# One list of lags, ranks by stage behind the first phase, and three small networks moved behind the last expert block

## The chip, the cores and the metric

The kernel runs on one core of one Trainium2 chip. The metric is the device time of one execution in microseconds, the median of several runs. The core's engines are PE (TensorE: matrix products and transpositions, with PEld for the loading of weights), DVE (VectorE), ACT (ScalarE), POOL (GpSimd) and SP, which here only issues DMAs. Each engine carries out its instructions strictly in the order in which they are written; an instruction that waits holds up everything behind it on its engine.

## The reference, cut to what matters

Two layers of a network over x of 32 sequences with 256 tokens of width 256 (8192 tokens), all in float32, 16 heads of 16. What the change touches begins in the last part of the first layer.

```python
# layer 0: modulated linear attention, gated cosine attention, adapter, attention block (the first phase), then
h = layer_norm(x); x = x + moe(h)          # 8 experts of width 1024, two choices a token, 2048 slots an expert, ReLU
# layer 1, "second linear" and the kernel attention
y = clip(((x * styles) @ weight.T) * dcoefs + bias, -256, 256)       # styles, dcoefs: one vector a sequence
q, k, v = y @ Wq.T + bq, y @ Wk.T + bk, y @ Wv.T + bv
q = q / norm(q); k = k / norm(k)           # norms over the whole tensor, all sequences together
s = sum(phi(q) * phi(k))                   # phi: exp of a small product, one s for each token and head
x = x + s * v / s
# layer 1, conditioning
h = ln(ln(x, pw[pathway]), cp[compartment]); t = ln(x, tm[time]); s = ln(x, ms[scale])   # gains, offsets gathered by token
m, n, r = (x + mlp_ln(state) for state in (memory, noise, resource))                     # one vector a sequence
w = softmax(aw)
c = ln(silu(concat(w0*h, w1*t, w2*m, w3*n, w4*r, w5*s) @ W1 + b1) @ W2 + b2)
# layer 1, feed-forward: 256 to 1024 to 256, both weights passed through ten butterfly stages
x = x + butterfly(gelu(butterfly(c @ W_exp + b_exp) + up_bias)) @ W_con + b_con + down_bias
```

## The kernel before, in words

**The planner.** The program is not written in the order in which it is executed. Each piece of work is a `Part`, a generator that yields an engine and a cost in microseconds ahead of the instructions it then writes (`yield PE, 1.75`). It can also yield a pause (`None, 2.0`), a join with another Part, a turn of a ring of buffers or of a set of lanes, a Part to be started beside it, and a change of rank. `side_by_side(parts, lags)` (L98) simulates the engines with these costs: of all steps that are due it takes the one with the earliest start, and among equal starts the one with the lowest rank; where a Part passes from one engine to another, a lag is added by the engine that it comes from. A step with two choices (`(ACT, 0.7), (DVE, 0.75)`) goes to the engine where it ends first. The order so found is the order of the instructions on each engine. It is fixed before anything runs, so a cost or a lag that is not that of the chip changes only the order. `DVE2` is a DVE operation that also takes the "port" which POOL operations take, so that the planner lays neither beside the other.

A Part's rank begins as its place in the list of Parts. `yield "stage", name` sets it to that place plus `STAGES[name]`; in the kernel before only the first phase does this. `yield "rank", B` puts the feed-forward of a sequence behind all earlier steps of others.

The first phase is planned by `side_by_side(..., LAGS_A)`, with a lag of 0.08 us, or 0.3 behind PE. All that follows is planned in a single call with `LAGS_D`, 0.2 us behind every engine:

```python
[routed, weights_part, *loads[:2], matrices, *blocks, *loads[2:], table_part, *first_parts, square_part, norm_part]
+ [Part(answer_out(b, first_parts[-3] if b < 2 else norm_part, [norm_part])) for b in range(B)]
```

**What follows the first phase**, in order of time:

- `expert_block` (32 blocks, 4 for each expert, 512 slots each; 4 lanes). POOL gathers the tokens (xg, L1600), PE transposes them (L1610), then 8 groups of bh (L1644) with a ReLU on ACT or DVE (L1633), then by (L1659), the sum ysb on DVE (L1665), the gate of the slot, and `add_to_tokens`: a POOL issue for each 128 slots that adds rows to `rrows` in DRAM (L1567), one at a time by `scatter_turn`.
- `matrices`, the butterflies: the 20 stages on w_eff and w_con, six DVE2 operations each (L1701 to L1707), which lie beside the expert blocks; at its end PE transposes w_con in four groups (L1761) and DVE copies them.
- `small_tables` joins `matrices` first. It loads rows, multiplies the phi weights (L1930, L1940), scales the conditioning weights iw1 on ACT and adds parts of them to wcat on POOL, and then carries out the three small networks for memory, noise and resource one after another, each with its loads, PE (L2008, L2017, L2034), ACT, DVE and POOL steps. A last group on PE (L2050) makes bvec of them.
- `answer(b)` (32 sequences, 6 lanes), the second linear: it waits for all blocks and scatters, loads x back, transposes it (xmT), multiplies by cw, clips to yT and stores that; 28 sequences add to a gram matrix, 4 make their squares directly.
- `squares` and `norms`: the norms of q and k over everything (L2069 to L2099). qs, a product with ones, rstd on POOL, scaled phi weights (wa_aq, ab_aq), aphr and phs. Every sequence's phi product waits for them. `norms` joins all `answer`s, `squares`, `small_tables` and `matrices`.
- `answer_out(b)` (4 lanes), the last stretch, one chain for each sequence:
  - dyT and x are loaded, and POOL gathers six rows of gains and offsets (`tables`, ga and gc, L2106);
  - v by wav on PE and DVE (L2152); the phi product on PE (L312) and ph on DVE (L2164), exp on ACT (L2167), sums on DVE (L2171 to L2181), x + v on POOL (L2183);
  - statistics (L361, L362) on DVE, rstd on POOL (L256, L262) and the norm on DVE (L284): xh; then t and s by two POOL operations each (L2118, L2120), and beside them hh by two on DVE, the second norm, h by two on DVE, its transposition on PE (L292) and its copy cT_h on DVE (L2205);
  - the wcat product on PE (L2218) over x, t, s and h; Silu on ACT (L2227), iw2 on PE (L312), u on DVE (L2235), its norm un, transposition and zT on DVE (L2246);
  - the feed-forward: four groups of dh (L2269) with Gelu on ACT (L2259), do (L2283), the sum xo on DVE (L2289) and the store.

Names such as `mm`, `sh` and `big` are rings of buffers, `mm` those in PSUM.

Of the kernel before, what the change touches and what calls it, by code (L numbers as in the profile page):

```python
# [93 lines left out]
LAGS_A = defaultdict(lambda: 0.08, {PE: 0.3})  # L94
LAGS_D = defaultdict(lambda: 0.2)


def side_by_side(parts, lags):  # L98
# [112 lines left out]
    "residual out": 0.0,  # L211
}
# [3 lines left out]
def network(ctx: ExitStack, tc: tile.TileContext, a: dict, out: bass.AP):  # L216
# [1140 lines left out]
    with tc.manual_schedule():  # L1357
        side_by_side(
            [tables[False, "k"], *first_sequences, Part(moderate()), Part(routed_early(first_sequences))]
            + [tables[False, "o"], constants_part, tables[True, "k"], tables[True, "o"], adapter_part, tables[False, "c"]]  # L1360
            + [Part(numbers())],
            LAGS_A,
        )
    with tc.If(nc.values_load(again[0:1, 0:1]) > 0):
        sequences = [Part(sequence(b, True)) for b in range(B)]
        side_by_side([*sequences, Part(routed_early(sequences))], LAGS_A)
# [184 lines left out]
    def slot_gates(j0):  # L1551
        for p in rest:
            yield "join", p
        yield None, 2.0
        yield POOL, 1.1 * QT_
        for j in range(j0, j0 + QT_):
            nc.gpsimd.indirect_dma_start(
                gslot[:, j : j + 1], None, gbuf[:, :], bass.IndirectOffsetOnAxis(ap=grow[:, j : j + 1], axis=0)
            )
        yield None, 2.0  # L1560

    def add_to_tokens(y, j0, n):

        for t in range(n):
            yield scatter_turn
            yield POOL, 1.6
            nc.gpsimd.indirect_dma_start(  # L1567
                rrows[:, :], bass.IndirectOffsetOnAxis(ap=row[:, j0 + t : j0 + t + 1], axis=0), y[:, t, :], None,
                compute_op=ALU.add,
            )  # L1570
            yield None, 3.0
            yield "back", scatter_turn
        yield back("sh")
# [15 lines left out]
    def expert_block(e, blk, w, loaded, routed):  # L1589
        yield lanes_b  # L1590
# [13 lines left out]
        yield None, 2.0  # L1604
        hT = []
# [17 lines left out]
        yield hid_turn  # L1623
        hid = []

        def relu(f, ps):
            bcol = cols[:, C_B1 + 8 * e + f : C_B1 + 8 * e + f + 1]
            o = hid[f // 4][:, f % 4, :]
            engine = yield (ACT, 0.7), (DVE, 0.75)
            if engine == DVE:  # L1630
                nc.vector.tensor_scalar(o, ps, bcol, 0.0, ALU.add, ALU.max)
            else:
                nc.scalar.activation(o, ps, AF.Relu, bias=bcol)  # L1633
            yield back("mm")
# [16 lines left out]
        for p in rs:  # L1651
            yield "join", p
        for t0 in range(0, QT_, 2):
# [57 lines left out]
    def butterflies(after):  # L1711
# [33 lines left out]
        for st in reversed(range(NST)):  # L1745
# [9 lines left out]
            yield back("big")  # L1755
        for f in range(0, 8, 2):
# [7 lines left out]
            yield DVE, 0.7  # L1764
            nc.vector.tensor_copy(w_con[:, f : f + 2, :], ps)
# [21 lines left out]
    def answer(b):  # L1787
# [3 lines left out]
        for p in scatters:  # L1791
            yield "join", p
        yield lanes_c
# [24 lines left out]
        if b < NG:  # L1818

# [80 lines left out]
    def small_tables():  # L1900

        yield "join", weights_part
        yield "join", matrices
        yield SP, 0.1
        nc.sync.dma_start(rowsD, a["rows_d"][:, :N_ROWS_D].to_broadcast([P, N_ROWS_D]))
        bb = yield from get("sh", "bb")
        yield SP, 0.1
        nc.sync.dma_start(
            bb.rearrange("p t d -> p (t d)"), a["rows_d"][:, N_ROWS_D : N_ROWS_D + 2 * D].to_broadcast([P, 2 * D])
        )  # L1910
        yield None, 2.5
        yield DVE2, 0.5
        nc.vector.tensor_add(bcon, bb[:, 0, :], bb[:, 1, :])
        yield back("sh")
        yield POOL, 0.1
        nc.gpsimd.memset(qacc, 0.0)
# [3 lines left out]
        nc.sync.dma_start(blk, a["ablk"].rearrange("(k p) m -> p k m", p=P))  # L1920
        for n in ("aq", "ak"):
            nat = yield from get("sh", "nat")
            yield SP, 0.1
            nc.sync.dma_start(nat, a[n].rearrange("(k p) i -> p k i", p=P))
            yield None, 2.5
# [20 lines left out]


# [7 lines left out]
        condin = {}  # L1955
        for n, src, k in (("mem", "condT", P), ("noi", "noiT", 64), ("res", "resT", 32)):
            if n == "mem":
                condin[n] = condT
            else:
                condin[n] = wD.tile([k, B], F, name="ci_" + n)  # L1960
                yield SP, 0.1
                nc.sync.dma_start(condin[n], a[src])
# [27 lines left out]
        vT = {}  # L1990
        for n in ("mem", "noi", "res"):
            ci = condin[n]
            k = ci.shape[0]
            m1 = yield from get("sh", "m1", [k, D])
            m2 = yield from get("sh", "m2")
            rb = yield from get("sh", "rb", [B, D])
            yield SP, 0.1
            nc.sync.dma_start(m1, a[n + "W1"])
            yield SP, 0.1
            nc.sync.dma_start(m2, a[n + "W2"].rearrange("(k p) n -> p k n", p=P))  # L2000
            o, w_ = ROWS_S[n + "b2"]
            yield SP, 0.1
            nc.sync.dma_start(rb, a["rows_s"][:, o : o + w_].to_broadcast([B, w_]))
            yield None, 2.5
            ps = yield from get("mm", "mm", TS)
            yield PE, 0.4
            for m in range(2):
                nc.tensor.matmul(ps[:, m, :B], m1[:, m * P : (m + 1) * P], ci, start=True, stop=True)  # L2008
            hT = yield from get("sh", "mhT", [P, 2, B])
            yield ACT, 1.8  # L2010
            for m in range(2):
                nc.scalar.activation(hT[:, m, :], ps[:, m, :B], AF.Silu, bias=col(n + "b1", m))
            yield back("mm")
            ps = yield from get("mm", "mm", TS)
            yield PE, 0.9
            for c in range(2):
                nc.tensor.matmul(ps[:B, 0, :], hT[:, c, :], m2[:, c, :], start=(c == 0), stop=(c == 1))  # L2017
            u = yield from get("sh", "mu", [B, D])
            st = sm.tile([B, 6], F, name="mst")
            mv = sm.tile([B, 2], F, name="mmv")  # L2020
            rstd = sm.tile([B, 1], F, name="mrs")
            yield DVE, 1.1
            nc.vector.tensor_add(u, ps[:B, 0, :], rb)
            nc.vector.bn_stats(st, u)
            nc.vector.bn_aggr(mv, st)
            yield back("mm")
            yield POOL, 0.8
            rsqrt(rstd, mv[:, 1:2], 1, LN_EPS)
            yield DVE, 0.4
            nc.vector.tensor_scalar(u, u, mv[:, 0:1], rstd, ALU.subtract, ALU.mult)  # L2030
            ps = yield from get("mm", "mm", TS)
            yield PE, 0.3
            for c in range(2):
                nc.tensor.transpose(ps[:, c, :B], u[:, c * P : (c + 1) * P], ident[:B, :B])  # L2034
            vT[n] = wD.tile([P, 2, B], F, name="vT_" + n)
            yield DVE, 0.3
            for c in range(2):
                nc.vector.tensor_scalar(
                    vT[n][:, c, :], ps[:, c, :B], col(n + "g", c), col(n + "be", c), ALU.mult, ALU.add
                )  # L2040
            yield back("mm")
            for _ in range(5):
                yield back("sh")
# [57 lines left out]
    def tables(b, gt):  # L2101
        for n, q in (("pw", 0), ("ct", 1), ("ms", 2)):
# [20 lines left out]
    def side_part(xh, gt, n, i, name, into):  # L2123
        x = yield from modulated(POOL, name, xh, gt, n, i, 1.3)
# [3 lines left out]
    def whole(x2, into):  # L2128
        into["x"] = yield from transposed(x2, "cT_x")

    def answer_out(b, begin, before):

        yield "join", begin
        yield lanes_d
# [21 lines left out]


# [9 lines left out]
        nc.scalar.activation(ph, ph, AF.Exp)  # L2167
        s_ = sm.tile([P, 2, H], F, name="s_")
# [17 lines left out]

        cT = {}
# [8 lines left out]
        hh = yield from modulated(DVE, "hh", xh, gt, "pw", 0, 0.7)  # L2196
        h2 = yield from layer_norm(sm, hh, "h2")
# [6 lines left out]
        yield DVE, 0.7  # L2204
        nc.vector.tensor_copy(cT["h"], ps)  # L2205
        yield back("mm")
        yield back("sh")
        for p in (px, pt, ps_):
# [35 lines left out]
        yield DVE, 0.9  # L2244
        for c in range(2):
            nc.vector.tensor_scalar(  # L2246
                zT[:, c, :], ps[:, c, :], col("intg", c), col("intbe", c), ALU.mult, ALU.add
            )
# [3 lines left out]
        yield "rank", B  # L2252
        gT = yield from get("big", "gT", [P, 8, S])

        def gelu(ps, f0):
            yield ACT, 1.0 if f0 else 2.2
# [20 lines left out]
        for p in gs:  # L2277
            yield "join", p
        ps = yield from get("mm", "do", [P, 2, D])
# [30 lines left out]
    norm_part = Part(norms([*first_parts, square_part, table_part, matrices]))  # L2310
    with tc.manual_schedule():
# [3 lines left out]
            LAGS_D,  # L2315
# [124 lines left out]
```

## Time and profile before

| what | value |
|---|---|
| median of 3 runs | 3712.47 us (3708.94 to 3715.06) |
| profiled execution, its own time | 3708.21 us |
| its span in the profile | 3706.5 us |
| mean granted TensorE clock | 0.978 |
| PE busy | 3488.0 us, 94% of the span |
| PEld busy | 2564.0 us, 69% |
| DVE busy | 2467.3 us, 67% |
| ACT busy | 1805.9 us, 49% |
| POOL busy | 1887.7 us, 51% |
| DMA | 241.44 MB, mean 65 GB/s |

The times of single instructions come from one profiled execution. A line of the timeline reads: start, duration, engine, source line, operation, output<-inputs, shapes, and in brackets the idle time of the engine before the instruction and what ended it. A line of the list of waits reads: instruction that waited <- instruction that released it: total us, how often, largest.

### The profile page before, as it was taken

The numbers are of one execution on the slowest core, as the hardware profiler recorded it, in microseconds if no ns is written. First come the engines' busy times: TensorE is split into PE (matmuls) and PEld (weight loads), VectorE is DVE, ScalarE is ACT, GpSimd is POOL, SyncE is SP. The second block draws the span as 40 slices with busy tenths as digits, with TensorE's granted clock in tenths as the row PEclk, the third lists the DMA queues.
The fourth block names the chain that finished last, engine by engine and source line by source line (L and its number), as shares of the span: only waits on it lengthen the run. The fifth ranks groups of instructions, "written<-read, shape, count | busy, mean of one in ns | idle before, by whom it ended". The sixth has DMA issues, their size and how long they took to land. (4 is left out here: it accounts for less than half of the span.)

```text
span 3706.5 us, 55576 instructions
## 1 busy us (share of the span) xinstructions
PE 3488.0 (94%) x22001; PEld 2564.0 (69%) x22001; DVE 2467.3 (67%) x4039; ACT 1805.9 (49%) x2790; POOL 1887.7 (51%) x1515
## 2 busy tenths in 40 slices
PE   3899999999999999969999999999998999999999
PEld 2566666666666666646666666666787888888888
DVE  7999999999999999747654540011346656565554
ACT  2677777777777777732222222222333333333333
POOL 4546555555555554426546665553024656565553
PEclk7999999999999999979999999999999999999999
DMA  1011010100100111032334334222341323233321
GB/s 64 16 34 33 31 31 31 31 31 27 29 25 28 31 31 37 25 123 69 101 83 106 97 76 91 44 37 40 131 168 43 105 93 116 94 97 97 120 94 43
DMA packets 136495, 241.44 MB, mean 65 GB/s; under 512 B 19265, under 2 KB 80897, under 8 KB 133666
## 3 DMA queue, kind: packets, MB, share of 16 engines
q0 software_dynamic: 48128, 100.77, 11.2%
q1 hardware_dynamic: 87954, 136.51, 11.1%
q8 instruction: 176, 2.88, 0.3%
q14 instruction: 93, 0.76, 0.1%
q10 hardware_dynamic: 144, 0.52, 0.0%
HBM read 187.25 MB, written 50.48 MB: 64 GB/s over the span
## 5 line engine op out<-in xcount | busy, mean ns | idle before, releaser
L1028 ACT ACTIVATE pt<-sc 128x2048 f32<-128x2048 f32 x256 | 481.5, 1881 | 108.6 <-PE sc L1019 105.7
L1633 ACT ACTIVATE hid<-bh,cols 128x512 f32<-128x512 f32 x256 | 175.3, 688 | 600.5 <-PE bh L1644 600.5
L1659 PE MATMUL by<-w,hid 128*128 128x256 f32 x2048 | 454.5, 380 | 3.2 <-DVE ysb L1665 3.2
L1644 PE MATMUL bh<-ehT,w 128*128 128x512 f32 x1024 | 451.5, 594 | 0.8 <-DVE ysb L1665 0.8
L1659 PEld LDWEIGHTS by<-w,hid 128*128 128x128 f32 x2048 | 387.7, 191 | 67.8 <-issue 14.3
L262 POOL TENSOR_TENSOR n<-n,negh 128x32 f32<-128x32 f32 x64 | 364.8, 5700 | 5.3
L1567 POOL DMA_INDIRECT rrows<-ysb,row x128 | 220.3, 1721 | 259.7 <-DMA rrows<-ysb,row 146.2
L1665 DVE TENSOR_TENSOR ysb<-by,b 128x512 f32<-128x512 f32 x64 | 44.0, 688 | 456.9 <-PE by L1659 382.7
L1644 PEld LDWEIGHTS bh<-ehT,w 128*128 128x128 f32 x1024 | 194.8, 191 | 220.8 <-issue 214.7
L256 POOL TENSOR_SCALAR rstd<-mv 128x2 f32<-128x2 f32 x160 | 62.7, 392 | 506.9 <-DVE mv L362 500.5
L835 DVE TENSOR_TENSOR hprod<-hprod 128x1024 f32<-128x1024 f32 (+2 forms) x384 | 313.3, 816 | 7.1
L1019 PE MATMUL sc<-qT,kT 32*128 32x256 f32 x4096 | 294.2, 401 | 19.4 <-ACT pt L1028 17.8
L827 DVE TENSOR_TENSOR hprod<-hex,kk 128x2048 f32<-128x2048 f32 x128 | 292.2, 2283 | 0.0
L1001 PE MATMUL av<-pt,vaug 128*32 128x256 f32 x4096 | 271.8, 385 | 5.6 <-ACT pt L1028 5.6
L1019 PEld LDWEIGHTS sc<-qT,kT 32*128 32x128 f32 x4096 | 185.4, 184 | 93.7 <-ACT pt L1028 42.7
L2269 PE MATMUL dh<-zT,w_eff 128*128 128x256 f32 x1024 | 235.9, 379 | 0.5 <-DVE zT L2246 0.5
L2283 PE MATMUL do<-w_con,gT 128*128 128x256 f32 x1024 | 230.9, 379 | 0.0
L1600 POOL DMA_INDIRECT xg<-h2buf,tok x128 | 149.3, 1167 | 156.8 <-issue 69.1
L256 POOL TENSOR_SCALAR n<-n 128x32 f32<-128x32 f32 x64 | 57.1, 892 | 300.7 <-DVE n L877 184.7
L2283 PEld LDWEIGHTS do<-w_con,gT 128*128 128x128 f32 x1024 | 192.0, 190 | 24.7
L2269 PEld LDWEIGHTS dh<-zT,w_eff 128*128 128x128 f32 x1024 | 189.9, 190 | 24.2 <-ACT cT_s L344 0.7
L1001 PEld LDWEIGHTS av<-pt,vaug 128*32 128x32 f32 x4096 | 108.0, 109 | 121.0 <-issue 54.1
(615 smaller groups left out, 7375.3 us busy)
## 6 DMA issues: line engine op xcount, KB each, us to landing
w<-in_w SPq DMA_DIRECT2D x16, 1024.0 KB, 8.2
x<-rrows SPq DMA_DIRECT2D x64, 256.0 KB, 3.1
bfw<-in_upw SPq DMA_DIRECT2D x10, 1024.0 KB, 6.9
bfw<-in_dnw SPq DMA_DIRECT2D x10, 1024.0 KB, 5.1
xT<-in_xT SPq DMA_DIRECT2D x32, 256.0 KB, 3.5
x<-in_x SPq DMA_DIRECT2D x32, 256.0 KB, 2.8
ugbb<-gtab SPq DMA_DIRECT2D x32, 256.0 KB, 3.8
h2buf<-xh SPq DMA_DIRECT2D x32, 256.0 KB, 2.5
```

What stands on the lines that cost most here:

```text
L262: nc.gpsimd.tensor_tensor(o, o, negh[:p].to_broadcast([p, n]), ALU.pow)
L827: nc.vector.tensor_tensor(pr.rearrange("p j (h d) -> p j h d", d=DH), weights(t, j0, 8)[:, 0].unsqueeze(3).to_broadcast([P, 8, H, DH]), wi ...
L835: nc.vector.tensor_tensor(pr[:, :n], pr[:, :n], pr[:, n : 2 * n], ALU.add)
L1001: nc.tensor.matmul(av[32 * i : 32 * i + 32, c % 2, :], va[:, kc, 4 * c + i, :], pt[:, i, kc, :], start=(kc == 0), stop=(kc == 1),)
L1019: nc.tensor.matmul(sc[:, i, kc, :], kT[r, m, kc * P : (kc + 1) * P], qT[r, e, m, :], start=True, stop=nm is None,)
L1028: nc.scalar.activation(pt, sc, AF.Exp, scale=1.0 / math.sqrt(DH))
L1567: nc.gpsimd.indirect_dma_start(rrows[:, :], bass.IndirectOffsetOnAxis(ap=row[:, j0 + t : j0 + t + 1], axis=0), y[:, t, :], None, compute_o ...
L1633: nc.scalar.activation(o, ps, AF.Relu, bias=bcol)
L1644: nc.tensor.matmul(ps, w["w1"][:, c, f * P : (f + 1) * P], hT[c], start=(c == 0), stop=(c == 1))
L1659: nc.tensor.matmul(ps[:, t, :], hid[f // 4][:, f % 4, (t0 + t) * P : (t0 + t + 1) * P], w["w2"][:, f, :], start=(f == 0), stop=(f == 7),)
L2269: nc.tensor.matmul(ps[:, g, :], w_eff[:, c, f * P : (f + 1) * P], zT[:, c, :], start=(c == 0), stop=(c == 1))
L2283: nc.tensor.matmul(ps[:, t, :], gT[:, f, t * P : (t + 1) * P], w_con[:, f, :], start=(f == 0), stop=(f == 7))
```

## The change

It does five things.

1. `LAGS_A` and `LAGS_D` become one `LAGS` with the numbers of the first phase (0.08, and 0.3 behind PE). The first phase is planned with the same numbers as before.
2. `STAGES` gets 21 names for what is behind the first phase, and the Parts there yield them.
3. The phi weights and the three small networks become Parts of their own (`phi_weights`, `condition_network`). `small_tables` joins `blocks[-4]` in place of `matrices`; the loads of these Parts are issued then, and their PE work joins the last expert block.
4. The transpositions of w_con join the first 30 `answer`s, and their copies go to ACT. `norms` no longer joins `matrices`; the feed-forward of each sequence does.
5. The copy cT_h and zT go to DVE or ACT, wherever the planner ends them first.

```diff
-LAGS_A = defaultdict(lambda: 0.08, {PE: 0.3})
-LAGS_D = defaultdict(lambda: 0.2)
+LAGS = defaultdict(lambda: 0.08, {PE: 0.3})
...
     "residual out": 0.0,
+    "experts": -6.0,
+    "slots of experts": 0.0,
+    "hidden": -1.0,
+    "answers of experts": -5.5,
+    "relu": 0.0,
+    "weights of slots": 0.0,
+    "additions": -4.5,
+    "second linear": 1.0,
+    "its products": 0.0,
+    "last in": -1.0,
+    "phi": 0.0,
+    "by phi": 0.5,
+    "conditioning": 1.0,
+    "norm of conditioning": 0.0,
+    "hidden state": 0.0,
+    "feed-forward": -0.5,
+    "feed-forward out": 0.5,
+    "tables": 2.5,
+    "sides": 0.5,
+    "itself": 1.5,
+    "gelu": -1.0,
...
 def butterflies(after):
...
+        for p in first_parts[: NG + 2]:
+            yield "join", p
         for f in range(0, 8, 2):
             ps = yield from get("mm", "mm", TS)
             yield PE, 0.55
...
-            yield DVE, 0.7
-            nc.vector.tensor_copy(w_con[:, f : f + 2, :], ps)
+            yield ACT, 0.6
+            nc.scalar.copy(w_con[:, f : f + 2, :], ps)
...
+    def phi_weights():
         blk = yield from get("sh", "blk", [P, 2, P])
...
+        nats = []
         for n in ("aq", "ak"):
             nat = yield from get("sh", "nat")
+            nats.append(nat)
...
-            yield None, 2.5
+        yield None, 2.5
+        yield "join", blocks[-1]
+        for n, nat in zip(("aq", "ak"), nats):
...
+    def condition_network(n, src, k, vT):
...
+        yield None, 2.5
+        yield "join", blocks[-1]
+        ps = yield from get("mm", "mm", TS)
+        yield PE, 0.4
+        for m in range(2):
+            nc.tensor.matmul(ps[:, m, :B], m1[:, m * P : (m + 1) * P], ci, start=True, stop=True)
...
+    def small_tables():
         yield "join", weights_part
-        yield "join", matrices
+        yield "join", blocks[-4]
...
+        vT = {}
+        nets = [Part(condition_network(*n, vT)) for n in (("mem", "condT", P), ("noi", "noiT", 64), ("res", "resT", 32))]
+        for p in nets:
+            yield p
+        phis = Part(phi_weights())
+        yield phis
...
+        for p in (*nets, phis):
+            yield "join", p
         ps = yield from get("mm", "mm", TS)
         yield PE, 1.6
...
     def answer_out(b, begin, before):
...
-        yield DVE, 0.7
-        nc.vector.tensor_copy(cT["h"], ps)
+        engine = yield (DVE, 0.7), (ACT, 0.6)
+        if engine == ACT:
+            nc.scalar.copy(cT["h"], ps)
+        else:
+            nc.vector.tensor_copy(cT["h"], ps)
...
-        yield DVE, 0.9
+        engine = yield (DVE, 0.9), (ACT, 1.0)
         for c in range(2):
-            nc.vector.tensor_scalar(
-                zT[:, c, :], ps[:, c, :], col("intg", c), col("intbe", c), ALU.mult, ALU.add
-            )
+            if engine == ACT:
+                nc.scalar.activation(
+                    zT[:, c, :], ps[:, c, :], AF.Identity, bias=col("intbe", c), scale=col("intg", c)
+                )
+            else:
+                nc.vector.tensor_scalar(
+                    zT[:, c, :], ps[:, c, :], col("intg", c), col("intbe", c), ALU.mult, ALU.add
+                )
...
         yield "rank", B
+        yield "join", matrices
+        yield "stage", "feed-forward"
...
-    norm_part = Part(norms([*first_parts, square_part, table_part, matrices]))
+    norm_part = Part(norms([*first_parts, square_part, table_part]))
...
-            LAGS_D,
+            LAGS,
```

The new `"stage"` lines are: in `expert_block` "experts" at its start, "slots of experts" ahead of the transpositions, "hidden" ahead of bh, "relu" and "answers of experts"; "weights of slots" and "additions" in the two Parts that it starts; in `answer` "second linear" and "its products"; in `answer_out` "last in" at its start, "phi" ahead of the phi product, "by phi" ahead of the sums, "conditioning" ahead of its norm, "norm of conditioning" ahead of the second norm, "hidden state" ahead of the wcat product, then "feed-forward", "gelu" and "feed-forward out"; "tables", "sides" and "itself" in the Parts that it starts.

## The prediction

> **What bounds the kernel now.** I read first the busy time of each engine by stretch of the span (columns: length, then PE, PEld, DVE, ACT and POOL busy, granted clock, DMA share, GB/s).
>
> ```profile
> 1666.00:2590.00 924.00, 919.11 (x3373) 616.75 (x3372) 356.87 (x497) 220.19 (x324) 498.46 (x372) 1.00 0.33 75
> 2590.00:2603.00 13.00, 0.48 (x3) 0.48 (x4) 1.07 (x7) 7.01 (x19) 6.03 (x7) 0.55 0.36 71
> 2603.00:2756.00 153.00, 152.30 (x881) 134.85 (x880) 56.64 (x128) 50.77 (x131) 15.77 (x45) 0.98 0.45 155
> 2756.00:2800.00 44.00, 26.16 (x104) 21.32 (x104) 35.99 (x75) 7.00 (x13) 31.61 (x33) 0.73 0.28 84
> 2800.00:3706.50 906.50, 887.12 (x4369) 771.62 (x4367) 510.22 (x1025) 331.69 (x542) 504.49 (x533) 1.00 0.29 92
> ```
>
> In the expert stretch PE works 919.1 of 924.0 us, in the second linear 152.3 of 153.0, in the last stretch 887.1 of 906.5. So PE sets the end, and the change can win only PE's pauses, or lose by making new ones. The pauses behind 2590 us: 13 us while the last scatters land, some 18 us in the stretch from 2756 to 2800, and 14.1 us of waits in the last stretch, of which the list of who waited for whom shows the largest:
>
> ```profile
> PE mm L292 <- DVE h L2120: 5.2, 6, 1.0
> PE mm L292 <- POOL s L2120: 3.8, 6, 1.8
> ```
>
> The other waits there (dyT 1.6, t 1.3, x 0.9, un, zT and hsT together 1.3) make the 14.1. The remaining lines are one batch's chain in the timeline, from its phi product on PE (L312, ph) to the transposition of h:
>
> ```profile
> 2926.03 1.89 PE L312 MATMUL mm<-wa_aq,dyT 128*128 128x256 f32 x8
> ...
> 2928.05 0.66 DVE L2164 TENSOR_TENSOR ph<-mm,aphr 128x512 f32<-128x512 f32 x1
> ...
> 2928.74 0.63 ACT L2167 ACTIVATE ph<-ph 128x512 f32<-128x512 f32 x1 [7.22 <-DVE ph L2164]
> ...
> 2935.54 1.28 POOL L2183 TENSOR_TENSOR x<-x,v 128x512 f32<-128x512 f32 x1
> 2936.85 0.43 DVE L361 BATCH_NORM_STATS2 st<-x 128x6 f32<-128x256 f32 x1 [2.08 <-POOL x L2183]
> ...
> 2938.39 0.73 POOL L262 TENSOR_TENSOR rstd<-rstd,negh 128x2 f32<-128x2 f32 x1
> ...
> 2940.88 0.69 DVE L2118 TENSOR_TENSOR hh<-dxh,ga 128x512 f32<-128x512 f32 x1
> 2940.92 1.77 POOL L2118 TENSOR_TENSOR t<-dxh,gc 128x512 f32<-128x512 f32 x1 [0.56 <-DVE dxh L284]
> ...
> 2941.60 1.64 DVE L2120 TENSOR_TENSOR hh<-hh,ga 128x512 f32<-128x512 f32 x1
> ...
> 2944.34 1.27 POOL L2118 TENSOR_TENSOR s<-dxh,ga 128x512 f32<-128x512 f32 x1
> ...
> 2945.68 1.26 POOL L2120 TENSOR_TENSOR s<-s,ga 128x512 f32<-128x512 f32 x1
> ...
> 2947.63 1.16 POOL L262 TENSOR_TENSOR rstd<-rstd,negh 128x2 f32<-128x2 f32 x1
> ...
> 2952.11 0.63 PE L292 MATMUL mm<-ident,h 128*128 128x128 f32 x4 [0.99 <-DVE h L2120]
> ```
>
> To be seen: PE must be given other work for as long as this chain runs; here 24 us passed and PE was 1.0 us short of work. POOL does t and s (four operations) before the rstd of the second norm, so that DVE's norm of h waits for s. And DVE's hh of L2120 took 1.64 us beside POOL's t, where the same shape took 0.69 alone (L2118).
>
> The profiled execution took 3708.2 us: its span of 3706.5 and 1.7 around it. The median of the runs is 4.3 above it, and I add that at the end.
>
> **The change part by part.** The first phase keeps its instruction order on every engine; everything differs from the first expert block on.
>
> *Networks and phi weights behind the last block.* Before, three small networks interrupt the second linear: PE 3 x about 0.5 (L2008), 3 x 0.98 (L2017) and two of three 0.24 (L2034), 4.9 us by start-to-start times. After, they stand between the last by and the first x, in the 13 us in which PE waits for the scatters: -4.9. Two phi groups of 0.45 leave the expert stretch for the same pause: -0.9, since the pause is measured from the half block that they preceded (its four scatters, at 4.5 us pitch, set it). On POOL the three rstd of the networks queue behind the last scatter issue (2595.96 + 1.55); 3 x 0.9 us later is 2600.2, before x lands at 2602.5. The third network's transposition is behind five x already, so at worst it costs 1 us. The Silu table load (1.28 us) falls into the pause too. SP issues their nine loads (three for each network) under the experts instead of between x loads (0.4 us each): nothing, while the experts cover it; if not, 3.6 us. The scaling of iw1 on ACT (twelve times 0.41 us), which had filled the pause, and wcat's additions on POOL (some 3 us in all) now come ahead of the last scatters, under the experts: ACT works 0.69 of each 0.86 us between two relus, so 2 us at the worst; I take 0.
>
> *w_con's transposes.* 4 x 0.44 us leave the experts and come back at the end of the second linear: 0. Their copies go from DVE (0.7) to ACT, idle there. `matrices` is now awaited by the feed-forward alone: the first dh (2815.4) comes some 65 us behind these copies, so this join is free.
>
> *Ranks in the experts.* The butterflies fall behind ysb on DVE. Before, one 3.2 us and one 0.8 us wait for ysb, and the half clock after the first (1.7): between 0 and -5.7; I take -4, as ysb now stands between single butterfly operations.
>
> *Norms.* Before, PE waited 0.8 for qs and 2.8 for ab_aq with nothing between; now a wav product of 1.73 us stands in each: -2.5. The half clock after those waits (6.8 us, of which PE worked about 4.5, so 2.2 lost) goes too: -2.2.
>
> *First four batches.* h of batch 0 waited 7.0 us, as DVE served batch 1 in between and POOL both its t and s. After, DVE takes batch 0's norm first; I count its transposition about 5 us earlier, but batch 2's h then has 13.9 us of PE work ahead of it against 16 of DVE rows: -4, between -8 and 0.
>
> Sum of these: -4.9 - 0.9 - 4 - 4.7 - 4 = -18.5 (-24 to -8).
>
> *Lags and ranks in the last stretch* decide. The new order on PE repeats every four batches (112 us, seven times). PE work between the end of ph and h was 20.8 to 27.2 us; it is now 16.45, 18.2, 17.7 and 17.7. The chain got shorter in the order: DVE serves one batch without others' work, and POOL does the rstd before s. Its rows: hop and ph 0.9, exp 0.65, sums 1.3, v twice 1.35, x on POOL 1.4, norm 1.2 + 1.1 + 0.8, hh 2.4, norm 1.2 + 1.1, norm of h, two products 1.4 and a hop 0.15. Only the norm of h lacks a row in this position: beside nothing it took 0.8, beside one POOL operation 1.7 (2948.82). Now POOL starts s with it, and one place of the first batches shows that:
>
> ```profile
> 2780.74 1.26 POOL L2118 TENSOR_TENSOR s<-dxh,ga 128x512 f32<-128x512 f32 x1
> 2780.77 2.72 DVE L284 TENSOR_SCALAR dxh<-x,mv,rstd 128x256 f32<-128x256 f32 x2
> ...
> 2782.08 1.26 POOL L2120 TENSOR_TENSOR s<-s,ga 128x512 f32<-128x512 f32 x1
> ```
>
> With 2.72 the chain is 17.7 us: 1.3 too long for the first batch of four. I walked the other three along the written orders. Second: its exp stands on ACT behind cT_s of the batch ahead and a table load, and starts 1.6 us late; short by 1.1. Third: POOL has four gathers (1.25 each) ahead of the rstd that un of the first batch needs, DVE has this un ahead of the third's sums; short by 1.6. Fourth: x waits behind five gathers, u and un come first; short by 2.35. Together 6.35 us in four batches, 44 in seven rounds, against 13.6 now: +31. Bounds: the bare chain alone (1.3 x 7 = 9, so -4.5), and the half clock behind the two larger waits of each round: the 3.2 us wait for ysb was followed by 3.4 us at 0.50, 1.7 lost, so +24 more, +55.
>
> The Trainium skill (SBUF — State Buffer, Who interferes with whom) states that a GpSimd operation and a DVE operation in a two-port mode lock each other out for the whole instruction. Strictly alternating, the pair of norm operations would take 1.27 + 0.41 + 1.27 + 0.41 = 3.4 instead of the 2.72 of the row: by the rule another +0.6 a batch, and 18 more in all; I keep to the row.
>
> *Copies on either engine.* 23 of 32 cT_h and 14 of 32 zT go to ACT (0.59 against 0.68, 1.0 against 0.99 us), which is 37% busy there: 0 by itself; DVE gets 30 us of room that PE does not need.
>
> Sum: 3708.2 - 18.5 + 31 = 3720.7, and 4.3: 3725 us.
>
> **The rivals.** *The order holds (faster).* If s on POOL starts late enough to leave h's norm alone, the chain is 15.8 us and under every gap; it decides at 16.45. Then only the bare or no waits remain: -18.5 - 4.5, 3689. For: the lags follow the rows (PE to DVE 0.2, others 0.03 to 0.15). Against: the 2.72, and gathers priced at 1.1 against 1.25.
> *Half of it.* Waits overlap, so that one pause of PE pays for two chains: +14 instead of +31, 3708; with the ramp gaining nothing, 3712. No change that a measurement of this kernel can tell (0.2%, 7.4 us).
> *The clock joins in.* The fourth batch's wait reaches 3 us and the granted clock falls each round: up to +24, 3749 at the most.
> *It does not do what it says.* The networks could hold x on PE if POOL's rstd came later than 2602; then 1 to 2 us of the 4.9 are lost, within my range.
>
> **How the numbers follow.** Forecast 42% (3725, its own range 3713 to 3740), the order holds 30%, half of it 16%, the clock 12%. The range from 3688 to 3754 leaves out the lower part of the second case, about 10 in 100, and the top of the last with the far bounds of the small terms, another 5 to 10. Faster by over 0.2%: 0.30; within: 0.16; slower: 0.42 + 0.12 = 0.54.
>
> **What would show it.** Right: PE's waits for h (now 5.2 us) rise to over 20 us behind 2800, with t beside them; DVE's norm of h lasts 2 us or more a pair; no wait for qs, and x's wait still near 13 us with L1987 and L1996 of the new file inside it. Wrong: waits for h under 10 us, POOL's s not beside DVE's norm, or a second linear no shorter than 150 us.

## The result, and the profile after

The changed kernel takes 3742.0 us (median of four runs, 3740.0 to 3743.6), the kernel before beside it 3713.8. The ratio is 1.0077 with a 95% interval of 1.0060 to 1.0095: 28 us slower. The forecast was slower too, 3725 us in a range from 3688 to 3754; the sum behind it had 12.5 us more where 28 came. The profiled execution took 3742.1 us, at its median; that of before took 3708.2, just below the four runs beside it (3708.9 to 3716.5). So the two spans lie 33.8 us apart, 3740.3 against 3706.5.

The list of who waited for whom on PE, behind 2800 us, of the changed kernel (total us, how often, longest):

```profile
PE mm L312 <- DVE h L2162: 38.4, 28, 2.4
PE mm L312 <- POOL t L2162: 8.4, 14, 0.9
PE mm L312 <- DVE un L304: 2.2, 1, 2.2
PE mm L332 <- DMA dyT<-ytbuf: 2.1, 3, 1.0
PE mm L312 <- POOL s L2162: 0.2, 1, 0.2
```

PE waited for h 28 times instead of 6, 38.4 us instead of 5.2, and for t 8.4 instead of 1.3. The waits for s, 3.8 us before, are gone, as rstd now stands ahead of s on POOL.

The busy time of PE in six rounds of four sequences, each from one transposition of h to the fourth behind it (columns: length, PE busy, granted clock, DMA share, GB/s):

```profile
2880.97:3003.58 122.61, 115.51 (x560) 0.99 0.30 95
3003.58:3125.62 122.04, 115.52 (x560) 0.99 0.31 95
3125.62:3245.71 120.09, 113.60 (x560) 1.00 0.31 97
3245.71:3367.55 121.84, 115.29 (x561) 0.99 0.31 95
3367.55:3488.86 121.31, 113.83 (x560) 1.00 0.32 96
3488.86:3611.36 122.50, 115.52 (x560) 0.99 0.31 95
```

A round takes 121.7 us on average. In the kernel before, six sequences take 172.5 us, which is 115.0 for four:

```profile
2952.00:3124.50 172.50, 170.46 (x840) 1.00 0.32 101
```

So a round costs 6.7 us more, 40 us in six rounds. Behind them nothing more is lost: from the h of the fifth sequence to the end it is 819.6 us in the kernel before and 859.3 now, 39.7 more in all. Where the clock was 1.00 throughout, PE is busy for 113.7 us in a round, as in the kernel before (113.6); in the other four rounds for 115.5, because the first products after a long wait (2.39 us at the start of the first round, 2.17 later in three others) run at half clock.

One chain in the timeline, the fourth sequence of a round:

```profile
3053.68 1.27 POOL L2230 TENSOR_TENSOR x<-x,v 128x512 f32<-128x512 f32 x1
...
3057.27 0.74 DVE L304 TENSOR_SCALAR dxh<-x,mv,rstd 128x256 f32<-128x256 f32 x2 [1.11 <-POOL rstd L282]
...
3061.98 0.70 POOL L282 TENSOR_TENSOR rstd<-rstd,negh 128x2 f32<-128x2 f32 x1
...
3062.66 1.27 POOL L2160 TENSOR_TENSOR s<-dxh,ga 128x512 f32<-128x512 f32 x1
3062.72 2.70 DVE L304 TENSOR_SCALAR h<-hh,mv,rstd 128x256 f32<-128x256 f32 x2 [1.10 <-POOL rstd L282]
...
3063.81 1.89 PE L2330 MATMUL dh<-zT,w_eff 128*128 128x256 f32 x8
3064.00 1.27 POOL L2162 TENSOR_TENSOR s<-s,ga 128x512 f32<-128x512 f32 x1
3065.22 1.32 POOL L2337 TENSOR_TENSOR x<-x,bcon 128x512 f32<-128x512 f32 x1
3065.46 1.63 DVE L2160 TENSOR_TENSOR h<-h,gc 128x512 f32<-128x512 f32 x1
...
3067.87 0.66 PE L312 MATMUL mm<-ident,h 128*128 128x128 f32 x4 [2.17 <-DVE h L2162]
```

The second rstd is out at 3062.68; POOL starts s and DVE the norm of h at the same moment. The two operations of the norm take 2.70 us, where the same norm of x, at 3057.27, took 0.74 while POOL stood between two operations. POOL's next addition then stretches the first product of h to 1.63. PE has dh ready until 3065.7 and waits 2.17.

By group, from 2900 to 3700 us (columns: count | total us, mean ns of one | idle before):

```profile
L304 DVE TENSOR_SCALAR h<-hh,mv,rstd 128x256 f32<-128x256 f32 x54 | 72.9, 1390 | 22.0 <-POOL rstd L282 22.0
...
L304 DVE TENSOR_SCALAR dxh<-x,mv,rstd 128x256 f32<-128x256 f32 x52 | 20.1, 426 | 29.1 <-POOL rstd L282 29.1
```

All 54 operations of the norm of h that lie there are slow, between 1.35 and 1.43 us each, where the norm of x takes 0.43 on average.

Ahead of that stretch the kernel did gain. On PE the first x product of the second linear starts 10.7 us earlier (2602.5, now 2591.9), ab_aq 7.1 earlier (2759.9, now 2752.8) and the first wcat product 16.0 earlier (2793.3, now 2777.2). But the h of the fifth sequence is only 5.9 us earlier (2886.9, now 2881.0).

### The profile page after: what moved, and what is told of

It reads as the page before. It is cut to its first block, busy times and chain, and to the rows that moved or that the text cites. A ratio compares the mean times of both kernels' runs of the same rounds, so it can differ in the third digit from the quotient of the medians.

```text
span 3740.3 us, 55619 instructions
## 1 busy us (share of the span) xinstructions
PE 3501.0 (94%) x22001; PEld 2571.7 (69%) x22001; DVE 2479.0 (66%) x3991; ACT 1815.6 (49%) x2825; POOL 1883.2 (50%) x1515
## 3 DMA queue, kind: packets, MB, share of 16 engines
q0 software_dynamic: 48128, 100.77, 11.5%
## 5 line engine op out<-in xcount | busy, mean ns | idle before, releaser
L1589 POOL DMA_INDIRECT rrows<-ysb,row x128 | 228.2, 1783 | 287.4 <-DMA rrows<-ysb,row 85.6
L1039 PE MATMUL sc<-qT,kT 32*128 32x256 f32 x4096 | 295.6, 403 | 18.5 <-ACT pt L1048 16.9
```

Of the source, the lines that this page charges most:

```text
L1039: nc.tensor.matmul(sc[:, i, kc, :], kT[r, m, kc * P : (kc + 1) * P], qT[r, e, m, :], start=True, stop=nm is None,)
L1589: nc.gpsimd.indirect_dma_start(rrows[:, :], bass.IndirectOffsetOnAxis(ap=row[:, j0 + t : j0 + t + 1], axis=0), y[:, t, :], None, compute_o ...
```

## The experiments

Each was timed in five rounds beside the kernel before, whose median lay between 3711 and 3715 us in all calls; the ratios below are to it. Each diff is against the changed kernel unless it says otherwise.

**The last stretch planned as before.** `p.lags` goes with a Part and with those it starts.

```diff
-            lag = 0.0 if uses[0] == p.engine else lags[p.engine]
+            lag = 0.0 if uses[0] == p.engine else (lags if p.lags is None else p.lags)[p.engine]
...
+        for p in outs:          # the answer_out Parts
+            p.lags = LAGS_D     # 0.2 behind every engine
...
-    "last in": -1.0,            # and the eleven other names of answer_out
+    "last in": 0.0,
...
-        engine = yield (DVE, 0.7), (ACT, 0.6)     # cT_h, and zT likewise
+        engine = yield DVE, 0.7
```

> The changed kernel, but answer_out planned as before: lag 0.2, no ranks by stage, both copies on DVE. PE's order in the last stretch is then that of the kernel before, with at least 20.8 us of PE work between the end of ph and h from the fifth sequence on. Theory (the new order of the last stretch costs what the rest gains and more): the gain up to the first wcat product, 16 us in the traces, stays, and the loss behind it goes: 3697 us, between 3692 and 3703, with h waiting some 1 us in six sequences as before. Rival (the loss comes from what the moved networks and transpositions push into the last stretch): 3720 us or more.

Measured: 3703.0 us, ratio 0.9971 (0.9959 to 0.9983), at the upper end of what was expected. The waits for h behind 2800 us are 5.2 us in six, as before. So the loss sits in the order of the last stretch, and the rest of the change is a gain of some 9 us.

**Ranks of the last stretch at zero.** The twelve values as above; new lags and free copies stay.

> The changed kernel with the twelve new ranks of the last stretch at 0.0, the new lags and the free copies kept. From the tenth sequence on the PE work between the end of ph and h is 19.5 and 27.2 us in turns, and POOL does s ahead of the second rstd again. Theory (it is the ranks that cut the work ahead of h to 16.45 to 18.2): the chain with s ahead of rstd needs 21.8 (20.8 of work and 1.0 of wait in the kernel before), so every second sequence waits 2.3 us, 14 waits or 32 us less what runs over: 3705 to 3730 us. Rival (the low lags make the loss, whatever the ranks): 3740 us as before the edit.

Measured: 3728.8 us, ratio 1.0044 (1.0030 to 1.0058). PE's waits behind 2850 us:

```profile
PE mm L312 <- POOL s L2162: 22.9, 12, 1.9
PE mm L312 <- POOL t L2162: 2.9, 7, 0.7
```

Twelve sequences wait 1.9 us each, where 14 waits of 2.3 were expected; but it is s that they wait for, and not h, and the norm of h is short here (0.45 us an operation). The time is in the range, by another wait than expected. The ranks are not the whole loss: without them the low lags still lose, and not by the norm of h beside s.

**Lags of 0.2, ranks kept.**

```diff
-            LAGS,       # second call of side_by_side
+            LAGS_D,     # 0.2 behind every engine
```

> The changed kernel with lags of 0.2 behind every engine in the second planner call, all ranks kept. The PE work between the end of ph and h is then mostly 19 to 23 us, with a few at 17.3 to 18.6, and POOL keeps rstd ahead of s. Theory (what counts is that this work covers a chain of 17.6 to 19.9 us, as measured by work plus wait in the changed kernel): waits for h in fewer than ten sequences, 1 us each, 3703 us, between 3695 and 3712. Rival (the ranks make the loss, whatever the lags): 3735 us or more.

Measured: 3745.8 us, ratio 1.0085 (1.0071 to 1.0099). My expectation failed, the rival's held. The longer lags did put 17.3 to 23 us of PE work ahead of h, but h waited 22.7 us in 16 sequences all the same, un 10.2 and s 9.8:

```profile
PE mm L313 <- DVE h L2163: 22.7, 16, 3.4
PE mm L313 <- DVE un L305: 10.2, 7, 2.7
PE mm L313 <- POOL s L2163: 9.8, 4, 3.1
```

Counting the work ahead of h did not foretell these waits: the norm of h met s here as well (1.39 us an operation). The ranks alone lose as much as ranks and lags together.

**A short s, order unchanged.** This kernel leaves s out; the instructions on PE and DVE follow one another as in the changed kernel.

```diff
+        if name == "s":
+            x = yield from get("sh", name)
+            for k in (i, i + 1):
+                yield POOL, 1.3
+                nc.gpsimd.tensor_tensor(x[:, :, :1], xh[:, :, :1], gt[n][:, :, k * D : k * D + 1], ALU.mult)
+            into[name] = yield from transposed(xh, "cT_" + name)
+            yield back("sh")
+            return
         x = yield from modulated(POOL, name, xh, gt, n, i, 1.3)
```

> The changed kernel with the computation of s left out: its two POOL operations touch one column instead of 256, and PE transposes xh in the place of s. Order of all engines as in the changed kernel. Theory (POOL's s beside DVE's norm of h makes that norm 2.7 us instead of 0.8, and this 1.9 us is what PE waits for): the norm of h falls to about 0.8 us, the waits for h of 1.2, 1.1, 0.9 and 2.2 us a round to 0, 0, 0 and about 0.3, and with them the half clock behind the last; t's 1.2 a round stays: some 6 us a round less, 3697 us, between 3690 and 3706. Rival (something else in the chain is as late, so that h waits all the same): above 3725 us.

Measured: 3685.8 us, ratio 0.9929 (0.9916 to 0.9943): 56 us less than the changed kernel and 4 us below the expected range. The norm of h (from 2900 to 3700 us) and PE's waits behind 2850 us:

```profile
L304 DVE TENSOR_SCALAR h<-hh,mv,rstd 128x256 f32<-128x256 f32 x52 | 19.1, 411 | 21.5 <-POOL rstd L282 21.5
```

```profile
PE mm L312 <- POOL t L2162: 2.2, 7, 0.3
PE mm L312 <- DVE h L2162: 1.9, 8, 0.4
```

The norm is back at 0.41 us an operation and the waits for h are 1.9 us in all. The same order that loses 28 us with the full s gains 27 without it.

**Powers in the place of s.** This kernel and the next keep POOL busy with an operation that is not a product.

```diff
-                nc.gpsimd.tensor_tensor(x[:, :, :1], xh[:, :, :1], gt[n][:, :, k * D : k * D + 1], ALU.mult)
+                nc.gpsimd.tensor_tensor(
+                    x[:, 0, :7], xh[:, 0, :7] if k == i else gt[n][:, 0, k * D : k * D + 7], negh.to_broadcast([P, 7]), ALU.pow
+                )
```

> The kernel with the short s again, but POOL is kept as busy as with the full one: each of the two operations of s is a power over 7 columns, by the rows about 1.26 us long (128x2 takes 0.71, 128x32 5.7), with a result that nothing reads. s is left out as there; the order is that of the changed kernel. Theory (it is where POOL's products and DVE's norm meet, and not POOL's time, that makes the norm of h long): a power beside the norm leaves it at 0.4 us an operation, and the time stays within 8 us of 3686. Rival (the short s helped by giving POOL 2.6 us a sequence for other work): 3715 us or more. A power that holds up DVE as a product does would also give 3730 to 3742, and then the norm stays at 1.4.

Measured: 3718.7 us, ratio 1.0011 (1.0002 to 1.0020); the number of the rival, but not its case. The powers took 1.48 and 2.02 us, 1.0 us a sequence longer than s, and PE waited 20.7 us for t and 8.2 for un, which POOL brought late. The norm of h beside them took 0.41. So they were cut to 6 and 5 columns of xh:

```diff
+                w = 6 if k == i else 5
                 yield POOL, 1.3
-                nc.gpsimd.tensor_tensor(x[:, :, :1], xh[:, :, :1], gt[n][:, :, k * D : k * D + 1], ALU.mult)
+                nc.gpsimd.tensor_tensor(x[:, 0, :w], xh[:, 0, :w], negh.to_broadcast([P, w]), ALU.pow)
```

> The kernel with powers in the place of s once more, over 6 and 5 columns of xh. The first powers took 1.48 and 2.02 us, 3.5 in all where s takes 2.5, so that POOL was busier by 1.0 us a sequence and t and un came late. By the rows of 2 and 7 columns (0.71 and 1.48) the new ones take 1.32 and 1.17, 2.5 in all. Theory (the place where POOL's products and the norm meet makes the loss, not POOL's time): the norm stays at 0.41 us an operation, the waits for t and un of 28.9 us shrink to those of the changed kernel, about 10, those for h stay below 4, and the time is 3690 us, between 3683 and 3702. Rival (half of the gain of the short s was POOL's time): 3710 us or more.

Measured: 3699.2 us, ratio 0.9966 (0.9952 to 0.9979). The powers, the norm of h beside them (both from 2900 to 3700 us), and PE's waits behind 2850 us:

```profile
L2172 POOL TENSOR_TENSOR s<-dxh,negh 128x6 f32<-128x6 f32 x26 | 34.3, 1321 | 0.0
...
L2172 POOL TENSOR_TENSOR s<-dxh,negh 128x5 f32<-128x5 f32 x26 | 30.3, 1167 | 2.0
```

```profile
L304 DVE TENSOR_SCALAR h<-hh,mv,rstd 128x256 f32<-128x256 f32 x52 | 19.1, 410 | 21.5 <-POOL rstd L282 21.5
```

```profile
PE mm L312 <- POOL t L2162: 15.6, 14, 1.3
...
PE mm L312 <- DVE h L2162: 0.7, 2, 0.4
```

POOL works 1.32 and 1.17 us beside the norm, as long as on s, and the norm is 0.41. Of the 56 us between the changed kernel and the short s, 43 go (3742.0 less 3699.2; 41 by the two ratios) with the same time of POOL: that is the meeting of POOL's products with DVE. In DVE's time the norm is most of it, 1.96 us a sequence; the first product of h is 0.24 us shorter as well (0.69 instead of 0.93 on average). The other 13 (3699.2 less 3685.8) are POOL's time; they show as the waits for t, 15.6 us, where I had expected 10 for t and un together.

**s on DVE behind h**, a version that leaves nothing out.

```diff
-        ps_ = Part(side_part(xh, gt, "ms", 0, "s", cT))
-        yield ps_
         hh = yield from modulated(DVE, "hh", xh, gt, "pw", 0, 0.7)
...
         yield from modulated(DVE, "h2", h2, gt, "ct", 0, 0.7, h2)
+        ps_ = Part(side_part(xh, gt, "ms", 0, "s", cT, DVE, 0.7))
+        yield ps_
```

> The changed kernel with s computed by DVE (two operations at 0.69 us) behind the two products of h, in place of POOL ahead of them. Nothing is left out. The planner makes a new order from it, with 16.4 to 23.8 us of PE work between the end of ph and h and 18.6 or more up to s. Theory (POOL's s beside the norm of h is the loss): the norm of h takes 0.4 us an operation, h is ready after some 16 to 18 us, waits for h stay below 10 us in all, and the time is near that of the kernel with the short s: 3690 us, between 3682 and 3702. Rival (DVE is the tight engine, so that 1.4 us more a sequence on it delay u, un and zT): above 3710 us.

Measured: 3725.8 us, ratio 1.0037 (1.0023 to 1.0051). The norm fell to 0.58 us an operation, but behind 2850 us h still waited 12.0 us in 15 sequences, s 11.5 and cT_h on ACT 3.5. The planner made another order, and that one found other late steps: the number expected for it was wrong, and the time is the rival's (above 3710), though the steps that the rival named (u, un and zT) are not those that PE waited for most.

**The same, with the last stretch planned as before.**

> The same move of s to DVE, in the kernel whose last stretch is planned as before (lag 0.2, no ranks there, copies on DVE). The work between ph and h is 18.2 to 23.4 us. Theory: the waits of 13.5 us behind 2850 us that were left in that kernel go nearly all, since POOL's s no longer stands ahead of the second rstd or beside a norm: 3703 less 11 is 3692, between 3685 and 3700. Rival (DVE is the tight engine): 3703 or more.

Measured: 3713.0 us, ratio 1.0000 (0.9991 to 1.0009), 10 us worse than without the move. PE waited 9.3 us for x + v and 6.7 for h. The rival held; whether DVE's load or the new order did it, these two runs do not tell.

**The norm of h on ACT.**

```diff
+            nc.vector.scalar_tensor_tensor(nb, mv[:, :, 0], -1.0, rstd, ALU.mult, ALU.mult)
+            yield ACT, 0.85
+            for t in range(2):
+                nc.scalar.activation(
+                    xh[:, t, :], x2[:, t, :], AF.Identity, bias=nb[:, t : t + 1], scale=rstd[:, t : t + 1]
+                )
```

> The changed kernel with the norm of h on ACT in place of DVE: DVE makes -mean times rstd (128x2), ACT does scale and bias for both halves (0.85 us). Nothing is left out; the planner makes a new order, with 19.9, 18.2, 19.9 and 23.8 us of PE work ahead of h in a round and 17.7 or more ahead of s. Theory (the norm beside POOL's s costs 2.7 us, the chain without it about 16 to 18): ACT does not meet POOL, the norm takes 0.9 us, h waits less than 5 us in all and the time is 3692 us, between 3683 and 3706. Rival (each new order finds another late step, such as un or s, as with s on DVE): 3715 us or more.

Measured: 3733.6 us, ratio 1.0054 (1.0040 to 1.0068). The rival held: h waited 30.2 us in 14 sequences, up to 4.3. An operation took 0.59 us on ACT, and the chain now has two more changes of engine and stands in ACT's queue.

**Copies on DVE alone.** The two `engine = yield` lines as in the first experiment.

> The changed kernel with the copy cT_h and zT on DVE alone. The order keeps rstd ahead of s; the PE work ahead of h is 16.4, 18.2, 17.7 and 19.9 us in a round, where it was 16.4, 18.2, 17.7 and 17.7. Theory (PE's waits are the chain's need less this work): the fourth wait of 2.2 us and the half clock behind it go, the others stay, some 3 us less in each of seven rounds: 3721 us, between 3712 and 3730. Rival (the free copies take load from DVE that h's chain needs): 3742 us or more.

Measured: 3736.2 us, ratio 1.0067 (1.0054 to 1.0081), 6 us better than the changed kernel; neither theory's number. Where the fourth wait was to go, the waits for h are 38.1 us in 28 and the longest 1.9: they were spread, not taken away. What went is the half clock: the granted clock was 1.00 throughout behind 2850 us, with waits that stay under 2 us.

**Old lags, no ranks, free copies** in the last stretch: the fourth corner.

> The changed kernel with answer_out planned with lags of 0.2 and ranks 0, but with the free copies: the fourth corner beside the changed kernel, the one with ranks 0 and the one with lags 0.2. h has 19.0 to 27.2 us of PE work ahead, s 15.1 to 23.4. Theory (old lags and no ranks together keep the order that covers the chain, the copies matter little): 3704 us, between 3698 and 3710. Rival (the free copies make part of the loss): 3714 us or more.

Measured: 3708.1 us, ratio 0.9982 (0.9973 to 0.9991). With the free copies, then: 3708 with neither, 3729 with low lags, 3746 with ranks, 3742 with both. The corner with ranks is not quite clean: there the lags of 0.2 hold in the whole second call, in the corner with neither in the last stretch alone. Both lose, the ranks more, and the losses do not add. Free copies cost 5 us here (3703.0 without).

**The networks alone.** Against the kernel before: `phi_weights` and `condition_network` as in the change, `small_tables` joining `blocks[-4]`, and nothing else.

> The kernel before with one part of the change alone: the three networks and the phi weights as Parts of their own behind the last expert block; lags, ranks, w_con's transposes, copies and joins as before. The last stretch has the order of the kernel before. Theory (they fit into the pause for the scatters): 4.9 us for the networks and 0.9 for the phi weights less, 3707 us, between 3703 and 3710. Rival (the gain up to the first x, 8 to 11 us in the traces, comes from here): 3701 us or less; or (their wait for the rstd on POOL holds the first x): 3712 us or more.

Measured: 3702.4 us, ratio 0.9971 (0.9961 to 0.9980): 10 us less by the medians, more than my 5.8 and just outside the range. The traces show less: ab_aq stands at 2756.5 instead of 2759.9, and the spans are 3701.7 and 3706.5, 4.8 apart. Half of the 10 us is thus what the profiled run of before lay under its median, and the traces can't show where that goes; how much of it the networks won is left open. The first x is at 2602.4, as before, so the gain is not ahead of it. The first experiment, which has all the other edits outside the last stretch as well, is no faster (3703.0). Of the kernels that compute all of the reference these two are the fastest; both beat the kernel before and the changed one.

## Why the prediction was right, and where its sum was off

**The bound** held. PE's waits behind 2850 us come to some 5 us in the fastest kernel here (3685.8 us), 49 in the changed one (3742.0) and 52 in the slowest (3745.8).

**The mechanism** held. h's norm beside POOL's s was read from one place of the trace of before, 2.72 us; it became the rule in the new order (two operations of 1.39), and the runs with the short s and with the powers show that some 42 us hang on the meeting of s with DVE's steps to h. The signs named for it came: 38.4 us of waits for h with 8.4 for t beside them, norms of 2.78 us a pair, and no wait for qs.

**The waits of a round** were forecast at 6.35 us. The timeline of one round (from 3003.6) shows 1.19, 1.09, 0.90 and 2.17 for h and 0.32 and 0.87 for t, 6.5. The split by sequence was less good: 1.3, 1.1, 1.6 and 2.35 were forecast, and with t counted to its sequence it is 1.2, 1.1, 1.2 and 3.0.

**Where the sum was off.** The profiled run lies 21.4 us above the sum (3742.1 and 3720.7). Counted at the fifth h, which came 5.9 us earlier where the first part of the sum had 18.5, 12.6 of these lie ahead of it, in the second linear and in the first four batches. The other 8.7 lie behind it, where 39.7 us were lost and the sum had 31.

**The half clock** is the term that was mis-sized behind the fifth h. I took it for a rival of 12 in 100, as the fourth wait was 2.35 by my count and not 3. That wait came to 2.17 us in each of the six rounds and once more behind them. Behind four of these seven waits the clock fell (0.67 on average in the 5.2 us that follow) and behind three it did not (1.00); it also fell behind the 2.39 us wait for the fifth h. Each time cost about 1.7 us of PE time. The waits themselves were nearer to the sum: from the fifth h on PE was idle 33.7 us longer than in the kernel before.

**The copies on either engine**, put at 0, cost 5 us with the old lags and no ranks (3708.1 and 3703.0) and 6 in the changed kernel (3742.0 and 3736.2), there together with the half clock.

**The second linear** with what stands around it, up to the first phi products, was forecast at -14.5; these ended 9.9 us earlier. The networks and the phi weights gave 5 us in the traces and 10 in the medians, where I had 5.8. The waits for ysb went (-4.0), and no wait for qs was left, but ab_aq kept 2.5 of its 2.8. And there was a wait that I had not priced. From the list of PE's waits between 2595 and 2800 us:

```profile
PE mm L318 <- DVE yT L1844: 4.8, 1, 4.8
...
PE mm L2128 <- DVE ab_aq L2124: 2.5, 1, 2.5
```

DVE stood still for 10 us, until 2706.1, and PE ran at half clock for 4.3 us behind its wait of 4.8, some 7 us lost together. So one sign of being wrong that the prediction named did come: from its first x product to the last of its products for the norms the second linear took 154.6 us (153.5 before), where under 150 was to be seen. In the time of the stop POOL issued ten gathers for the first sequences and the DMA engines were busy throughout (0.95 to 1.03 from 2692 to 2704). The kernel before issued the same ten in a row with the DMA engines as busy, and its DVE did not stop. The stop of 10 us is in all kernels here that plan this stretch with the low lags, and in none of the three that plan it with 0.2 (the kernel before, the one with the networks alone, and the one with lags of 0.2 and ranks kept, which differs from the changed kernel in the lags only). So it came with the low lags; what DVE waited for the trace does not name.

**The first four batches** were forecast at -4. The first wcat product did come 16.0 us earlier, and h of the first sequence by about as much, but behind it PE waited 1.45 and 2.39 us for h and 2.24 for un, with half clock after the last two. By the fifth h 10.1 of the 16.0 us were given back. From the first phi products (9.9 earlier) to the fifth h (5.9 earlier) this stretch cost 4.0 us. That step failed in its sign.

**The rival that said faster** had the point right at which it decides, 16.45 us of work against the chain without the meeting: the short s is that case. That it came to 3686 us where the rival said 3689 is luck in part: the short s also frees 13 us of POOL's time (3699 us without that), and the gain of 18.5 us, which the rival counts in full, was 10.0 us there by the fifth h (2886.9 before, 2876.9 with the short s). The rival needed s to start late enough, and nothing in the order made it do so.

**The Trainium skill** (SBUF — State Buffer, Who interferes with whom) states a lock for the whole instruction; with strict alternation my estimate from it for the pair of norm operations was 3.4 us. Measured: 2.78 (twice 1.39), nearer to the row of 2.72. And a power of POOL over 6 columns, 1.32 us long, did not hold up the norm beside it at all (0.41); so here the rule of the page does not hold for every POOL operation, and what the norm waits for is not the length of the POOL instruction as such. That hh's second operation takes 1.65 us beside t, in all 26 cases here, agrees with the page's statement that a DVE operation with two inputs in SBUF also contends.

**The median of before**: I added 4.3 us for what its profiled run lay under the median. The changed kernel's profiled run lay at the median, so this term belonged to the difference, not to the forecast of the new kernel; it shortens the miss by luck.

## What to carry to other kernels

A planner that packs a chain more tightly makes its steps meet: look where two engines that hold each other up will now start at the same moment, take the price of that meeting from whatever single place of the old trace shows it, and multiply it by the rounds. Count a wait that comes once a round together with the slow clock that may follow it. An experiment that keeps the order and only empties one operation tells such a cause apart; moving that operation to another engine does not, since the planner then makes a new order with late steps of its own.

## What was not expected of the hardware

A POOL operation lengthens DVE's norm when it is a product over 128x512 (1.39 us against 0.41) but not when it is a power over 128x6 of the same length (1.32 us beside 0.41). The length of a power on POOL differs with its input: over 7 columns, 1.48 us on normed values and 2.02 on gathered gains.
